# The second FFN layer of a parallel transformer block in seven block products, with its weights streamed from DRAM

## The chip, the cores and the metric

The kernel runs on one core of one Trainium2 chip. The metric is the device time of one execution in microseconds (us), lower being better; before the change it is 2092.24 us, the median of two runs (2092.05 and 2092.44). The engines named below are PE (matrix products), DVE (vector), ACT (scalar), POOL (GpSimd) and SP, which issues nearly all DMAs. Each engine works through its own list of instructions in order, and waits where an operand or a buffer is not ready.

## The reference

For 16 sequences of 512 tokens with 256 features: layer normalisation, then eight-head causal attention and a three-layer feed-forward network (FFN) side by side, both added to the input. The FFN's weights are booleans that stand for +1 and -1.

```python
def _conn_dense(kernel_bool, x):
    w = jnp.where(kernel_bool, jnp.float32(1.0), jnp.float32(-1.0))
    return x @ w
h = jnp.concatenate([x, -x], axis=-1)
h = s0 * _conn_dense(k0, h)          # 512 -> 1024
h = jax.nn.relu(h) * 2
h = s1 * _conn_dense(k1, h)          # 1024 -> 1024
h = jax.nn.relu(h) * 2
h = s2 * _conn_dense(k2, h)          # 1024 -> 256
...
xn = _layernorm(x, axis=-1)
x = x + _L0_attn_ref(xn, wq, wk, wv, wo) + _L0_ffn_ref(xn, k0, k1, k2, s0, s1, s2)
```

## The kernel before

**Batches and slots.** The 16 sequences are called batches `b`, the 8 heads `h`. One head of one batch is a slot, `g = 8b + h`, 128 slots in all. A slot scores head g row block by row block (`score_row`, L500: PE product `s`, DVE masked row minimum, ACT exponential, DVE reciprocal, POOL scaling), transposes its probabilities block by block (`turn`, L520: DVE, then a trip through DRAM, `bounce_p` out and `pT` back), projects q and k of head g+1 (`project_qk`, L457), multiplies probabilities and values of head g-1 (`attend`, L562), and adds the output projection of head g-2 to the sums `y` (`project_o`, L596). Around that, pieces of the FFN and of the next batch's layer norm are laid by hand.

**Who sets the order.** PE, SP and POOL run in the order in which the code issues (manual scheduling, L843). DVE and ACT are ordered by the framework; `behind` (L245) ties some of their instructions to a slot. An order once built is fixed.

**Rope.** `rotate` (L395) turns q and k: ACT copies with the halves swapped, DVE multiplies by the cosine, POOL by the sine (L405), POOL adds (L407). On POOL the order in a slot is: row block 0, sine of q, sum qT, row blocks 1 and 2, sine of k, row block 3, sum kT. The next slot's first score product needs that kT.

**Seven products.** q, k and v are already computed as 2x2 blocks in seven products in Strassen's manner (`seven_products`, L421), on PSUM tiles `pa` and `pb`. ACT copies intermediate states `ca`, `cb`, `cu` out before PE accumulates on, DVE adds the rest. The weights' sums (`w7_sb`, `wv7_sb`) are made once and stay in SBUF.

**FFN.** A float32 activation is split into two parts of the faster type fp32r, `h` and `l` (high and low), each multiplied by the same exact weights. Layer one, `ffn0(b, f)` (L619), makes one of eight feature blocks of 128: four products of 512 columns, then ACT makes the high part with a ReLU (L634) and DVE the low part (L635), both from PSUM. Layer two, `ffn1(b, f)` (L638), makes one output block with 16 products of 512 columns (eight chunks, two parts, L642); layer three, `ffn2` (L655), adds 8 products of 256 columns to `y` (L588). Eight blocks f of layer two lie in the eight slots, one slot late: each slot holds one block. `slot_of_head_0` (L718) holds all of layer one for its batch, `slot_of_head_1` (L774) and `slot` (L815) the rest. PSUM tiles of the products come from a pool `mm` of three.

**DMA.** SP sends, in each slot: the bounce out, four pT back, one `w1` block of 512 KB for layer two (`load_w1`, L158). The pT transfers wait for the bounce to land; everything after them on SP waits too. w1 was made from booleans in batch 0 (`make_w1`, L229) and written to `w1_dram`. All other weights stay in SBUF.

Of the kernel before, what the change touches and what calls it, by code (L numbers as in the profile page):

```python
# [22 lines left out]
def kernel(  # L23
# [92 lines left out]
    w7_sb = wpool.tile([P, 7, HD], F32, tag="w7", name="w7_sb")  # L116
# [4 lines left out]
    wv7_sb = wpool.tile([P, 7, NG, VN], F32, tag="wv7", name="wv7_sb")  # L121

    def load_w(engine, sb, w, h0, h1):
        engine.dma_start(
            sb[:, :, h0 * D : h1 * D],
            w[:, h0:h1, :].rearrange("(c p) h d -> p c (h d)", p=P),
        )

    def load_wk(engine, h0, h1):
        load_w(engine, w7_sb[:, WK0 : WK1 + 1 : WK1 - WK0], wk, h0, h1)  # L130
# [6 lines left out]
    k2_sb = hpool.tile([P, NF1, M], U8, tag="h1l", name="k2_sb")  # L137
    wo_sb = wpool.tile([P, H, M], F32, tag="wo", name="wo_sb")

    k1s, w1s = {}, {}
    w1_dram = dram.tile([NF1, P, NF0, P], F32, tag="w1", name="w1_dram", bufs=1)

    def load_k1(f):
        k1s[f] = wpool.tile([P, NF0, P], U8, tag="k1", name=f"k1_{f}", bufs=2)
        nc.sync.dma_start(k1s[f], k1.rearrange("(c p) f -> p c f", p=P)[:, :, ts(f, P)])

    def load_wv(gv):
        for c, places in enumerate(((A11, A21), (A12, A22))):  # L150
            nc.sync.dma_start(
                wv7_sb[:, places[0] : places[1] + 1 : places[1] - places[0], gv],
                wv[ts(c, P), gv * VH : (gv + 1) * VH, :].rearrange(
                    "p (i h) d -> p i (h d)", i=2
                ),
            )

    def load_w1(b, f):  # L158

        if (b, f) == (1, 0):  # L160
            nc.sync.dma_start(w1_dram[NF1 - 1], w1s[0, NF1 - 1].bitcast(F32))
        if 0 < b < B:
            w1s[b, f] = wpool.tile([P, NF0, P], F32R, tag="w1", name=f"w1_{b}_{f}", bufs=2)
            nc.sync.dma_start(w1s[b, f].bitcast(F32), w1_dram[f])
        elif b == 0:
            if f:
                nc.sync.dma_start(w1_dram[f - 1], w1s[0, f - 1].bitcast(F32))
            if f + 1 < NF1:
                load_k1(f + 1)

    load_w(nc.sync, w7_sb[:, WQ0 : WQ1 + 1], wq, 0, 2)
    load_wk(nc.scalar, 0, 2)
    nc.sync.dma_start(cos_sb, cos_t)
    nc.scalar.dma_start(sin_sb, sin_t)
    load_wv(0)
# [4 lines left out]
    for h0, h1 in ((2, 4), (4, H)):  # L180
        load_w(nc.sync, w7_sb[:, WQ0 : WQ1 + 1], wq, h0, h1)
        load_wk(nc.sync, h0, h1)
    load_k1(0)
    for gv in range(1, NG):
        load_wv(gv)
    xs[1] = load_x(1)
    nc.sync.dma_start(wo_sb, wo.rearrange("h d m -> d h m"))
    nc.sync.dma_start(k2_sb, k2.rearrange("(c p) f -> p c f", p=P))
# [14 lines left out]
    w2_sb = wpool.tile([P, NF1, M], F32R, tag="w2", name="w2_sb")  # L203
    sg_sb = cpool.tile([P, 3], F32, tag="sg", name="sg_sb")
    sg2_sb = cpool.tile([P, 3], F32, tag="sg2", name="sg2_sb")
    nsg_sb = cpool.tile([P, 3], F32, tag="nsg", name="nsg_sb")
    ab_sb = cpool.tile([P, 3], F32, tag="ab", name="ab_sb")
    c_sb = cpool.tile([P, 1], F32, tag="c", name="c_sb")

    def make_scales():  # L210
        neg = small.tile([P, 3], F32, tag="neg", name="neg", bufs=1)
        nc.vector.tensor_scalar(neg, s_sb, 0.0, None, ALU.is_lt)
        nc.vector.tensor_scalar(sg_sb, s_sb, 0.0, None, ALU.is_gt)
        nc.vector.tensor_tensor(sg_sb, sg_sb, neg, ALU.subtract)
        nc.vector.tensor_scalar(sg2_sb, sg_sb, 2.0, None, ALU.mult)
        nc.vector.tensor_scalar(nsg_sb, sg_sb, -1.0, None, ALU.mult)
        nc.vector.tensor_tensor(ab_sb, s_sb, sg_sb, ALU.mult)
        nc.vector.tensor_scalar(c_sb, ab_sb[:, 0:1], ab_sb[:, 1:2], 8.0, ALU.mult, ALU.mult)
        nc.vector.tensor_tensor(c_sb, c_sb, ab_sb[:, 2:3], ALU.mult)
# [9 lines left out]
    def make_w1(f, reduced, raised):  # L229
        t = w1s[0, f] = wpool.tile([P, NF0, P], F32R, tag="w1", name=f"w1_0_{f}", bufs=2)  # L230
        if f % 2:
            behind(nc.scalar.activation(
                t, k1s.pop(f), AF.Identity, bias=nsg_sb[:, 1:2], scale=sg2_sb[:, 1:2]
            ), raised)
        else:
            behind(nc.vector.tensor_scalar(
                t, k1s.pop(f), sg2_sb[:, 1:2], sg_sb[:, 1:2], ALU.mult, ALU.subtract
            ), reduced)

    def make_w2(reduced):  # L240
        behind(nc.vector.tensor_scalar(
            w2_sb, k2_sb, sg2_sb[:, 2:3], sg_sb[:, 2:3], ALU.mult, ALU.subtract
        ), reduced)
# [139 lines left out]
    def project_v_directly(b, gv):  # L383
        new_v(b, gv)
        for c in range(NT):
            pv = ps_mm.tile([P, T], F32, tag="mm", name=f"pv_{b}_{gv}_{c}")
            for i, places in enumerate(((A11, A12), (A21, A22))):
                for m in range(NM):
                    nc.tensor.matmul(  # L389
                        pv[:, ts(i, VN)], tokens(xnTs[b], m)[:, c], wv7_sb[:, places[m], gv],  # L390
# [18 lines left out]
    def project_qk_directly(g, engine):  # L409

        for name, places in (("q", (WQ0, WQ1)), ("k", (WK0, WK1))):
            pq = ps_mm.tile([P, T], F32, tag="mm", name=f"p{name}_{g}")
            for m in range(NM):
                nc.tensor.matmul(  # L414
                    pq, w7_sb[:, places[m], ts(g, D)], tokens(xnTs[0], m),
                    start=(m == 0), stop=(m == NM - 1),
                )
# [3 lines left out]
    def seven_products(name, b, product):  # L421
# [13 lines left out]
        t = tts[b]  # L435
        product(pa[:, :n], A11, xn_half(b, 0, 0), start=True, stop=False)
        product(pa[:, n:], A12, xn_half(b, 1, 0), start=False, stop=True)
        ca = work.tile([P, T], F32, tag="ca", name=f"ca_{name}", bufs=1)
        nc.scalar.copy(ca, pa)  # L439
        product(pb[:, n:], S1, t[:, 0], start=True, stop=False)  # L440
        product(pb[:, :n], A22, t[:, 3], start=False, stop=True)
# [3 lines left out]
        product(pa[:, :n], S2, t[:, 1], start=False, stop=False)  # L445
# [3 lines left out]
        product(pb[:, n:], S4, xn_half(b, 1, 1), start=False, stop=True)  # L449
        product(pa[:, :n], A21, t[:, 2], start=False, stop=True)  # L450
# [3 lines left out]
             cb.rearrange("p (i t) -> p i t", i=2)),  # L454
        )

    def project_qk(g):  # L457
# [5 lines left out]
        def product(out_, place, right, **marks):  # L463
            nc.tensor.matmul(  # L464
                out_, w7_sb[:, place, ts(h, D)], right, skip_group_check=True, **marks
            )

        for sums in seven_products(f"qk_{g}", b, product):
# [11 lines left out]
    def project_v(b, gv, t):  # L480
# [6 lines left out]
        def product(out_, place, right, **marks):  # L487
            nc.tensor.matmul(  # L488
                out_, right[:, t], wv7_sb[:, place, gv], skip_group_check=True, **marks
            )  # L490

        for sums in seven_products(f"v_{b}_{gv}_{t}", b, product):
# [69 lines left out]
    def attend(g):  # L562
# [7 lines left out]
        nc.vector.tensor_copy(oT, po)  # L570
# [25 lines left out]
    def project_o(g):  # L596
        b, h = divmod(g, H)
        for _ in add_y(b, oTs.pop(g), wo_sb[:, h, :]):
            pass
# [17 lines left out]
    h0s, h1s = {}, {}  # L617

    def ffn0(b, f):  # L619
        if f == 0:  # L620
            h0s[b] = [
                hpool.tile([P, NF0, T], F32R, tag=f"h0{n}", name=f"h0{n}_{b}") for n in "hl"
            ]
        ph = ps_mm.tile([P, T], F32, tag="mm", name=f"ph0_{b}_{f}")
# [8 lines left out]
        hi, lo = h0s[b][0][:, f, :], h0s[b][1][:, f, :]  # L633
        nc.scalar.activation(hi, ph, AF.Relu)  # L634
        nc.vector.scalar_tensor_tensor(lo, ph, 0.0, hi.bitcast(F32), ALU.max, ALU.subtract)  # L635
        yield

    def ffn1(b, f):  # L638
        ph = ps_mm.tile([P, T], F32, tag="mm", name=f"ph1_{b}_{f}")
        for c in range(NF0):  # L640
            for i in range(2):
                nc.tensor.matmul(  # L642
                    ph, w1s[b, f][:, c], h0s[b][i][:, c, :],
                    start=(c == 0 and i == 0), stop=(c == NF0 - 1 and i == 1),
                )
                if c < NF0 - 1 or i == 0:
                    yield
        hi = hpool.tile([P, T], F32R, tag="h1h", name=f"h1h_{b}_{f}")
        lo = hpool.tile([P, T], F32R, tag="h1l", name=f"h1l_{b}_{f}")
        nc.scalar.activation(hi, ph, AF.Relu)  # L650
        nc.vector.scalar_tensor_tensor(lo, ph, 0.0, hi.bitcast(F32), ALU.max, ALU.subtract)
        h1s[b, f] = (hi, lo)
        yield

    def ffn2(b, f):  # L655
        for r in h1s.pop((b, f)):
            yield from add_y(b, r, w2_sb[:, f, :])
# [12 lines left out]

# [3 lines left out]
    def scale_first():  # L674
        for places, scale, engine in (
            ((WQ0, WQ1), Q_SCALE, nc.gpsimd), ((WK0, WK1), K_SCALE, nc.scalar),
        ):
            for place in places:
                cols = w7_sb[:, place, : 2 * D]
                if engine is nc.scalar:  # L680
                    engine.mul(cols, cols, scale)
                else:
                    engine.tensor_scalar(cols, cols, scale, None, ALU.mult)

    def make_w7(w, scale1, scale2, reduced=None, raised=None, engine=nc.vector):

        for place, scale in ((A22, -scale2), (A21, scale2), (A11, scale1), (A12, scale1)):
            if scale != 1.0:
                behind(nc.scalar.mul(w[place], w[place], scale), raised)
        for out_, a, c in (  # L690
            (S1, A21, A22), (S2, S1, A11), (S4, A12, S2), (A21, A11, A21)
        ):
            tied = reduced if engine is nc.vector else None
# [238 lines left out]
```

## Time and profile before

| What | Value |
|---|---|
| median of two runs | 2092.24 us |
| profiled execution: its time, its span | 2091.51 us, 2089.7 us |
| granted TensorE clock | 0.999 |
| DVE, ACT, POOL busy, share of span | 67%, 52%, 49% |
| DMA: bytes of the SP queue, share of 16 engines | 281.34 MB, 45.3% |

A batch in the middle, by the starts of the first score product of each slot (the timeline of PE, us from the span's start):

| Slot (head) | start | length |
|---|---|---|
| 0 (all of layer one) | 1046.95 | 22.11 |
| 1 (half of a v projection) | 1069.06 | 15.83 |
| 2 (v) | 1084.89 | 16.72 |
| 3 (v) | 1101.61 | 16.72 |
| 4, 5, 6 | 1118.33 | 41.10 together |
| 7 (v) | 1159.43 | |

"Busy" is time in which an engine has an instruction in flight; for PE, whose products are pipelined, the distance from start to start is the cost, and mean durations overlap. An "idle before" with an arrow names what the engine waited for.

### The profile page before, as it was taken

To read this page: it belongs to the slowest core of one execution; us is meant where nothing else is said; L and a number is where in the kernel's file an instruction comes from. 1 tells how busy PE (TensorE), PEld (TensorE's weight loads), DVE (VectorE), ACT (ScalarE), POOL (GpSimd) and SP (SyncE) were. 2 spreads that over 40 slices of the span, in tenths; PEclk is the share of its full clock that TensorE was granted. 3 is DMA by queue.
4 is the path that set the end of the run, shared out by engine and by line. 5 is a ranking of instruction groups with operands and counts; after the bars stand their busy time and mean duration, and the time that the engine had idled before them with its cause. 6 is when DMAs were issued, how large, how long until landed. Compare 5 with 4: busy or idle time off the path is not lost.

```text
span 2089.7 us, 30265 instructions
## 1 busy us (share of the span) xinstructions
PE 2075.6 (99%) x9856; PEld 1730.4 (83%) x9856; DVE 1399.6 (67%) x3653; ACT 1084.7 (52%) x2418; POOL 1023.7 (49%) x1090
## 2 busy tenths in 40 slices
PE   8999999999999999999999999999999999999999
PEld 5888888888888888888888888888888888888887
DVE  7767666676666766667666676766667666676654
ACT  6555555555545555455554555555555554555543
POOL 5754445545454454444544455444554545545443
PEclk9999999999999999999999999999999999999999
DMA  6544535445444354444435444454453544534344
GB/s 181 158 141 125 159 111 155 129 126 149 124 139 139 123 142 126 149 139 122 143 114 161 127 136 130 126 159 116 137 148 113 153 116 140 158 114 139 106 139 129
DMA packets 162158, 284.33 MB, mean 136 GB/s; under 512 B 25168, under 2 KB 126544, under 8 KB 162000
## 3 DMA queue, kind: packets, MB, share of 16 engines
q1 hardware_dynamic: 160976, 281.34, 45.3%
q8 instruction: 78, 1.28, 0.3%
q10 hardware_dynamic: 1024, 1.05, 0.2%
q14 instruction: 80, 0.66, 0.1%
HBM read 178.00 MB, written 104.33 MB: 135 GB/s over the span
## 4 chain that ended last, share of the span: by engine, by line
PE 98%; DVE 1%; POOL 0%; DMA 0%; issue 0%; ACT 0%; SPq 0%; POOLq 0%; DVEq 0%; ACTq 0%
PE ph L642 22%; PE y L588 16%; PE po L543 13%; PE s L505 13%; PE pa_qk L464 10%; PE pb_qk L464 8%; PE ph L627 6%; PE pa_v L488 5%; PE pb_v L488 4%; PE pv L389 0%; DMA w_sb<-in_L_attn_wq_dram 0%; PE pq L414 0%; PE pk L414 0%; POOL w_sb L694 0%; DVE p L508 0%
## 5 line engine op out<-in xcount | busy, mean ns | idle before, releaser
L516 POOL TENSOR_SCALAR p<-p,rl 128x128 f32<-128x128 f32 (+3 forms) x512 | 296.9, 585 | 730.7 <-DVE rl L515 725.9
L642 PE MATMUL ph<-h0h,w 128*128 128x512 f32 x1024 | 519.7, 507 | 0.0
L642 PE MATMUL ph<-h0l,w 128*128 128x512 f32 x1024 | 411.3, 402 | 0.0
L505 PE MATMUL s<-kT,qT 128*128 128x128 f32 (+3 forms) x1024 | 359.3, 432 | 0.3 <-POOL kT L407 0.2
L513 ACT ACTIVATE p<-p,least 128x128 f32<-128x128 f32 (+3 forms) x512 | 286.4, 560 | 123.2 <-DVE least L508 118.1
L405 POOL TENSOR_TENSOR swq<-swq,sin_sb 128x512 f32<-128x512 f32 x127 | 197.7, 1557 | 297.3 <-ACT swq L400 295.8
L524 DVE STREAM_TRANSPOSE z<-p 128x128 f32<-128x128 f32 (+3 forms) x512 | 242.2, 493 | 93.4 <-POOL p L516 89.6
L543 PEld LDWEIGHTS po<-pT,v 128*128 128x128 f32 x1536 | 271.1, 190 | 37.6
L543 PE MATMUL po<-pT,v 128*128 128x256 f32 (+1 forms) x1536 | 298.6, 344 | 0.0
L508 DVE CUSTOM_DVE_ANT_0 p<-s,causal 128x128 f32<-128x128 f32 (+3 forms) x512 | 243.8, 484 | 14.9 <-PE s L505 14.9
L642 PEld LDWEIGHTS ph<-h0h,w 128*128 128x128 f32 x1024 | 193.1, 189 | 73.1 <-issue 26.9
L642 PEld LDWEIGHTS ph<-h0l,w 128*128 128x128 f32 x1024 | 193.3, 189 | 72.7 <-issue 26.8
L588 PE MATMUL y<-wo_sb,oT 128*128 128x256 f32 x1024 | 241.7, 379 | 0.0
L505 PEld LDWEIGHTS s<-kT,qT 128*128 128x128 f32 x1024 | 193.4, 189 | 33.7 <-POOL kT L407 0.6
L588 PEld LDWEIGHTS y<-wo_sb,oT 128*128 128x128 f32 x1024 | 193.9, 189 | 28.7
L439 ACT COPY ca_qk<-pa_qk 128x512 f32<-128x512 f32 x126 | 73.7, 585 | 274.4 <-PE pa_qk L464 274.4
L650 ACT ACTIVATE h1h<-ph 128x512 fp32r<-128x512 f32 x128 | 76.5, 597 | 253.0 <-PE ph L642 245.6
L515 DVE RECIPROCAL rl<-l 128x1 f32<-128x1 f32 x512 | 78.8, 154 | 142.3 <-ACT p L513 139.8
L407 POOL TENSOR_TENSOR kT<-kT,swk 128x512 f32<-128x512 f32 x127 | 169.4, 1334 | 0.1
L407 POOL TENSOR_TENSOR qT<-qT,swq 128x512 f32<-128x512 f32 x127 | 163.8, 1290 | 10.0
L405 POOL TENSOR_TENSOR swk<-swk,sin_sb 128x512 f32<-128x512 f32 x127 | 166.4, 1310 | 0.0
L399 ACT COPY swq<-q 64x512 f32<-64x512 f32 x126 | 77.9, 618 | 169.9 <-DVE q L474 169.9
(113 smaller groups left out, 3571.5 us busy)
## 6 DMA issues: line engine op xcount, KB each, us to landing
bounce_p<-z SPq DMA_DIRECT2D x128, 640.0 KB, 2.9
pT<-bounce_p SPq DMA_DIRECT2D x512, 160.0 KB, 3.3
w<-w_dram SPq DMA_DIRECT2D x120, 512.0 KB, 5.0
x_sum<-in_L_attn_x_dram SPq DMA_DIRECT2D x16, 512.0 KB, 6.1
x<-in_L_attn_x_dram SPq DMA_DIRECT2D x60, 128.0 KB, 6.2
bounce_x<-zx SPq DMA_DIRECT2D x15, 512.0 KB, 6.5
xnT<-bounce_x SPq DMA_DIRECT2D x60, 128.0 KB, 5.8
out_dram<-x_sum SPq DMA_DIRECT2D x15, 512.0 KB, 4.4
```

The lines of the kernel that those rows point to most:

```text
L405: engine.tensor_tensor(sw, sw, sin_sb, ALU.mult)
L407: engine.tensor_tensor(rt, rt, sw, ALU.add)
L464: nc.tensor.matmul(out_, w7_sb[:, place, ts(h, D)], right, skip_group_check=True, **marks)
L488: nc.tensor.matmul(out_, right[:, t], wv7_sb[:, place, gv], skip_group_check=True, **marks)
L505: nc.tensor.matmul(ps[:, :n], qT[:, ts(ic, P)], kT[:, :n], start=True, stop=True)
L508: reduced = nc.vector.tensor_tensor_reduce(out=p, in0=ps[:, :n], in1=causal[:, T - n :], scale=1.0, scalar=3e38, op0=ALU.add, op1=ALU.min, ...
L513: raised = nc.scalar.activation(p, p, AF.Exp, bias=least, scale=-1.0, accum_out=l)
L516: nc.gpsimd.tensor_scalar(p, p, rl, 1.0, ALU.mult, ALU.mult)
L524: behind(nc.vector.transpose(zs[:, :, block(ic, 0) : block(ic + 1, 0), :].rearrange("p j c a -> p c j a"), p.rearrange("p (c j a) -> p c j ...
L543: nc.tensor.matmul(po[:, (ics[0] - first) * P : (ics[-1] + 1 - first) * P], v[:, jc], pT[:, :, at[0] : at[-1] + 1 : max(at[-1] - at[0], 1) ...
L588: nc.tensor.matmul(ys[b][c // 2][:, c % 2, :], lhsT[:, ts(c, P)], rhs, start=(y_done[b][c] == 0 and c % 2 == 0), stop=(y_done[b][c] == N_Y ...
L642: nc.tensor.matmul(ph, w1s[b, f][:, c], h0s[b][i][:, c, :], start=(c == 0 and i == 0), stop=(c == NF0 - 1 and i == 1),)
```

## The change

1. **Layer two in pairs.** `ffn1(b, i)` makes blocks i and i+4 together in seven block products. Each is 4 chunks x 2 parts of 256 columns: 56 products of 256 columns for two blocks, where 32 of 512 columns stood. The four pairs lie in slots 2, 4, 5 and 7 (`PAIR_SLOTS`); slots 0, 1, 3 and 6 hold none. ffn2 of a pair (16 products) is in the slot after it.
2. **Sums of the activations.** `ffn0` keeps only the ReLU on ACT, into a float32 tile `h0r` of eight 256-column places. New `split_h0(b, c)`, four times in slot 0, makes four differences on POOL, then for the three plain and the four difference places the high part on ACT and the low part on DVE. `h0r` shares its buffers (one for even, one for odd chunks) with the layer-two weights.
3. **Sums of the weights.** In batch 0 each pair's seven weight blocks are made (ACT, DVE, POOL) and written to DRAM in two parts: A11, A12, S1, A22 (1 MB) and S2, S4, A21 (768 KB). Later batches load both parts of a pair. The first part is loaded in the slot before the pair, placed on SP ahead of that slot's bounce; the second at the beginning of the pair's own slot (pair 0), or of the slot after the previous pair's.
4. **Other weights streamed.** q and k weights with their sums: 448 KB for each slot; v weights: 896 KB, two for each batch; `wo`: 128 KB for each slot; `w2`: 256 KB for each pair. None stays in SBUF.
5. **Smaller.** The copy of the attention output (`oT` in `attend`) goes from DVE to ACT. Loads of x and the statistics for a batch are made earlier by several slots. All sums of weights are on POOL.

```diff
-    def ffn1(b, f):
-        ph = ps_mm.tile([P, T], F32, tag="mm", name=f"ph1_{b}_{f}")
-        for c in range(NF0):
-            for i in range(2):
-                nc.tensor.matmul(
-                    ph, w1s[b, f][:, c], h0s[b][i][:, c, :],
-                    start=(c == 0 and i == 0), stop=(c == NF0 - 1 and i == 1),
-                )
...
+    def split_h0(b, c):
+        hi, lo = (t[:, c] for t in h0s[b])
+        r = h0rs.pop(c)
+        for out_, p, q in ((T1, X12, X11), (T2, X22, T1), (T3, X22, X12), (T4, T2, X21)):
+            nc.gpsimd.tensor_tensor(r[:, out_], r[:, p], r[:, q], ALU.subtract)
+        for part in (slice(X11, T1), slice(T1, X12)):
+            nc.scalar.copy(hi[:, part], r[:, part])
+            nc.vector.tensor_tensor(
+                lo[:, part], r[:, part], hi.bitcast(F32)[:, part], ALU.subtract
+            )
+
+    def ffn1(b, i):
+        hi, lo = h0s[b]
+        def product(out_, place, x, start, stop):
+            for c in range(NC):
+                for n, t in enumerate((hi, lo)):
+                    nc.tensor.matmul(
+                        out_, w1s[b, i, place][:, c], t[:, c, x], start=start and not c + n,
+                        stop=stop and c == NC - 1 and n == 1, skip_group_check=True,
+                    )
+        for sums in seven_products(f"h_{b}_{i}", product):
+            if sums is None:
+                yield
...
+        nc.vector.tensor_tensor(first, *sums[0], ALU.add)
+        nc.vector.tensor_tensor(second, *sums[1], ALU.add)
+        nc.vector.tensor_tensor(both, *sums[2], ALU.add)
+        for t, r in enumerate(copies):
+            nc.scalar.activation(h1h[:, t], r, AF.Relu)
+            nc.vector.scalar_tensor_tensor(
+                h1l[:, t], r, 0.0, h1h[:, t].bitcast(F32), ALU.max, ALU.subtract
+            )
...
+    PAIR_SLOTS = (2, 4, 5, 7)
+    def begin(g):
...
+            load_w7(g + 2)
+        if g <= N_SLOTS:
+            load_wo(g - 1)
...
+            else:
+                load_w1(b, behind_pair + 1, 1)
...
+        if i is not None:
+            load_w2(b, i)
+        if h == 2:
+            if b:
+                load_w1(b, 0, 1)
+                load_wv7(b, 1)
...
     def slot_of_head_0(g):
...
                 some(qk, 1)
-                rest(l0[ic - 2])
+                rest(l0[(ic - 2) * NC])
         rest(qk)
         turn(g, reduced)
+        split_h0(b, 0)
         project_o(g - 2)
-        rest(l0[2], l0[3])
+        rest(l0[1], l0[NC + 1])
+        split_h0(b, 1)
         attend(g - 1)
...
+        rest(l0[2], l0[NC + 2])
+        split_h0(b, 2)
+        rest(l0[3], l0[NC + 3])
+        split_h0(b, 3)
```

## The prediction

> **What bounds the kernel now.** I read in this order: the page's busy shares, its chain of waits, PE's waits, then PE and POOL slot by slot in the timeline, and last the DMA by microsecond.
>
> ```profile
> span 2089.7 us, 30265 instructions
> ...
> PE 2075.6 (99%) x9856; PEld 1730.4 (83%) x9856; DVE 1399.6 (67%) x3653; ACT 1084.7 (52%) x2418; POOL 1023.7 (49%) x1090
> ...
> PE 98%; DVE 1%; POOL 0%; DMA 0%; issue 0%; ACT 0%; SPq 0%; POOLq 0%; DVEq 0%; ACTq 0%
> ```
>
> PE bounds everything; in steady state it never waits. Two prices come from the chain around 1000 us (start, length, what):
>
> ```profile
> 1003.65 0.93 PE y L588 x8
> 1005.88 0.92 PE ph L642 x4
> ```
>
> A 512-column fp32r product costs 0.230 us, a 256-column one 0.93/8 = 0.117: half the width is half the price, though each loads other weights. One 256-column float32 product (two records) costs 0.43, a slot's four scores 0.22, 0.43, 0.65, 0.86.
>
> But POOL is nearly as tight within a slot. The slot of head 6 starts at 1016.53 (its first score):
>
> ```profile
> 1020.66 1.57 POOL L405 TENSOR_TENSOR swq<-swq,sin_sb 128x512 f32<-128x512 f32 x1 [2.15 <-ACT swq L400]
> ...
> 1027.47 1.26 POOL L407 TENSOR_TENSOR kT<-kT,swk 128x512 f32<-128x512 f32 x1
> ...
> 1030.23 0.38 PE L505 MATMUL s<-kT,qT 128*128 128x128 f32 x2
> ```
>
> kT is ready 12.2 us after the slot's start; the slot lasts 13.7. The one short slot of the startup shows the limit, 12.1 us after the previous first score (37.64):
>
> ```profile
> 49.77 0.49 PE L505 MATMUL s<-kT,qT 128*128 128x128 f32 x2 [0.20 <-POOL kT L407]
> ```
>
> **The change part by part.**
>
> *PE.* Layer two: 2048 x 0.230 = 471 us goes, 3584 x 0.117 = 419 comes: 52 us gained, all on the bounding engine; nothing else of PE changes. PE alone would need per slot, adding instructions by these prices: slot 0 18.4, slot 1 12.1, 2 15.6, 3 17.0, 4 15.6, 5 17.5, 6 11.0, 7 18.6: 125.8 us for a batch, before 129.2. I now ask of each slot what else must fit.
>
> *Slot 6.* PE needs 11.0, POOL's chain 12.2 to 12.6 (the third score stays, the fourth comes 0.8 later behind the output projection). It takes 12.4: 1.4 lost.
>
> *Slots 0 and 1.* `split_h0` issues 16 POOL differences of 128x256. The nearest row, the weight sums of batch 0, gives four in 3.2 us (POOL, L694, 3.04 to 3.38). So 12.8 us of POOL follow kT in slot 0. High parts: eight ACT copies of 768 and 1024 columns; nearest rows: 1134 ns for 1024 (L224), 0.71 for 512 from SBUF (L352); so 0.86 and 1.13. Low parts: DVE 256 and 512 columns take 0.42 and 0.69, so 0.96 and 1.23. ReLU 0.60 as now.
>
> The instruction order of the changed program decides. ACT reads: ReLU of block 1; high differences of chunk 0; ReLU 5; both high copies of chunk 1; oT; ReLU 2; ReLU 6; plain copy of chunk 2; ReLU 3; high differences of chunk 2; ReLU 7; ca of the next q/k; both high copies of chunk 3; only then cb of the next q/k and the exponential. So ReLUs that POOL needs stand behind copies that need POOL, and PE's three PSUM tiles are emptied by those ReLUs. With the slot's first score at 0: kT at 11.8, as now; split 0 ends 15.0, its copy 16.2, ReLU 5 16.85; split 1 (16.9 on) 19.3, copy 20.5, oT 21.1, ReLU 2 21.7, ReLU 6 22.3; split 2 24.9, copy 26.1, ReLU 7 26.7; ca 27.3, split 3 29.1, copy 30.3, cb 30.9. PE: block 3 waits for ReLU 5, block 7 for ReLU 2, the next pb for ReLU 3 (23.8), so slot 1 starts at 24.7, not 18.4; its first q/k accumulation waits for ca, S4 for cb, and q/k end at 31.8, where PE alone would be at 21.6. From there sine of q starts 1.7 later (as in the fence) and kT follows 8 later: slot 2 starts at 41.6, PE alone 30.5.
>
> DVE's low parts read two SBUF operands beside POOL's differences. The row:
>
> ```profile
> L372 DVE TENSOR_TENSOR tt<-xnT 128x256 f32<-128x256 f32 x32 | 32.9, 1031 | 0.0
> ...
> L372 DVE TENSOR_TENSOR tt<-xnT,tt 128x256 f32<-128x256 f32 x16 | 6.4, 399 | 0.0
> ```
>
> The same work takes 1031 ns where POOL is busy and 399 where not. [...] Slots 0 and 1 take 43 us (bounds 38 and 48); now they take 37.9. DVE's and ACT's load alone (28 and 30 of 30.5 us) would nearly fill PE's time too.
>
> *Slot 2, DMA.* The second weight part of pair 0 can be loaded only here, its buffer having held h0r. On SP stand before it: pT of slot 1, which waits for that slot's bounce, then the output, w7, wo, w2. In slot 1 the last transpose comes 0.7 after row block 3, kT 1.3 after it, so the bounce leaves 0.5 us before slot 2 starts, not 3.6 as now (1081.25 against 1084.89). The bounce takes 2.9; at +2.4 pT begins; 0.66+0.52+0.46+0.13+0.26+0.79 = 2.8 MB must move. What such a burst moves:
>
> ```profile
> 1085.00:1086.00 1.00, 1.00 (x9) 0.95 (x8) 0.94 (x4) 0.86 (x2) 0.00 (x0) 1.00 0.72 189
> 1086.00:1087.00 1.00, 1.00 (x9) 0.95 (x8) 0.16 (x1) 0.47 (x3) 0.38 (x1) 1.00 1.05 260
> 1087.00:1088.00 1.00, 1.00 (x6) 0.87 (x5) 0.81 (x2) 0.30 (x1) 0.00 (x0) 1.00 1.01 215
> 1088.00:1089.00 1.00, 1.00 (x5) 0.75 (x4) 1.00 (x3) 0.96 (x3) 0.00 (x0) 1.00 1.07 316
> 1089.00:1090.00 1.00, 1.00 (x5) 0.75 (x4) 1.00 (x4) 0.99 (x2) 0.97 (x1) 1.00 1.13 424
> 1090.00:1091.00 1.00, 1.00 (x6) 0.84 (x6) 1.00 (x2) 0.82 (x3) 0.92 (x2) 1.00 0.84 324
> ```
>
> The last column is GB/s: mean 288 over 6 us with all engines busy. So 9.7 us plus about 1 to start and finish: +13. PE needs S2 at +7.2: 6 us lost. [...] I take the trace, 6 (bounds 2 and 8). Over a batch the loads are no bound: 14.9 MB of weights instead of 4.2 make some 450 MB, at 281.34 MB in 45.3% about 73% of the engines' time.
>
> *Pair slots 4, 5, 7 and slot 3.* ACT gains ca, cb, cu (1.5 us) per pair, DVE three adds and two low parts of 0.69 to 0.86 (3 us) where two low parts stood; 9 us lie between the last score and the first y product that needs them: nothing lost. Second parts of later pairs are sent a slot ahead or, in slot 5, some 2 us early by the same rate: nothing; if slower, 1 us each. The oT copy (0.69 on DVE, 0.6 on ACT) is covered by the slot until its y product; in slot 0 it is counted above. w7, wo and w2 come a slot ahead and are hidden; uncovered, each costs 2 to 5 us.
>
> *Sum of a batch.* 43 + 21.6 + 17.0 + 15.6 + 17.5 + 12.4 + 18.6 = 145.7, before 129.2: 16.5 longer, 15 times: 247 us.
>
> *Batch 0.* POOL additionally makes w7 (4 sums of 128 columns, about 1.8 us each head), v sums 3.2 twice, w1 sums 4 x 1.3 for each pair. In slots 0 and 1: 1.8 x 2 and 3.2 more among the splits, then 10 behind kT that hold up sine of q in slot 2; slot 6 starts behind 7. By the same reckoning slot 2 starts near 71 us instead of 49.77, slot 8 about 30 later than now, less what its own pairs save. I take 28 (bounds 12 and 40). The tail saves 2.
>
> Total: 2089.7 + 247 + 28 - 2 = 2363 as span; the run's own time is 1.8 above its span, the median 0.7 above that. Of two estimated stalls I have more room to err downwards; I put 2355.
>
> **The rivals.** *All is hidden (faster).* If the low-priority work found gaps as it does now (PE waits 9 us in the whole run), only PE counts: 2092 - 52 = 2040. For it: DVE reached 12.1 busy of 13.7 us in slot 6 without a stall. Against: ACT's fixed order. It decides where the four splits, from kT to cb, take under about 8 us; I count 19. Chance 8%.
>
> *The gain is spent (within 2%).* Slots 0 and 1 lose 3, slot 6 1, slot 2 nothing, batch 0 10: about 2060 to 2110. Chance 6%.
>
> *One of two.* Only the POOL and ACT chain (slot 2 in time: 15 x 6 less, 2265) or only the weights (15 x 12 less, 2175). Between 2134 and 2265; 19%.
>
> *Both, as forecast.* 2265 to 2450: 67%. A half-width product that costs more than half, so that the change gives no PE time, is spoken against by the y row; it would add 52.
>
> **How the numbers follow.** 2% is about what a measurement of this kernel tells from no change: below 2050 faster, above 2134 slower. Faster 0.08, same 0.06, slower 0.86. The range from 2190 to 2430 leaves out the first two cases and the low end of the third, and a few in a hundred above.
>
> **What would show it.** In the profile after: PE busy share clearly below 99%; PE waiting for ACT at layer one (ReLU) and at q/k S4 in slots 0 and 1, about 10 us a batch; the L706 groups on POOL at 0.75 to 1.0 us each; PE waiting for the DMA of the second weight part in slot 2; slot 6 waiting for kT; slot 2 beginning 41 to 45 us after slot 0. I am wrong if slots 0 and 1 take under 34, or if no product waits for a weight transfer.

## The result and the profile after

The changed kernel takes 2497.19 us (median of 2 runs, 2496.5 to 2497.89), 1.1935 times the time before (95% interval 1.1884 to 1.1987): 405 us more, where the forecast was 263 more. The sign and the two stalls that the forecast named were right; the size was not, and two further losses were not in it.

The page of the changed kernel: span, busy shares, the granted clock in 40 slices, the chain by engine.

```profile
span 2496.1 us, 35132 instructions
...
PE 2191.5 (88%) x11392; PEld 1822.4 (73%) x11392; DVE 1595.6 (64%) x3726; ACT 1368.0 (55%) x2884; POOL 1294.4 (52%) x1380
...
PEclk8998999999999899998999989999998999989999
...
PE 46%; POOL 17%; ACT 11%; DVE 10%; DMA 8%; issue 6%; SPq 1%; ACTq 0%; POOLq 0%; DVEq 0%
```

PE, 98% of the chain before, is 46% of it now; POOL, ACT, DVE and DMA are links of the chain. The clock row has 8s, where a granted clock of 1.0 would show 9s. What PE waits for (total us, times, longest):

```profile
PE ph L689 <- ACT h0r L696: 100.2, 31, 12.5
PE pa_h L720 <- DMA w<-w_dram: 87.8, 20, 6.5
PE pb_qk L517 <- ACT cb_qk L487: 37.1, 18, 2.6
PE s L558 <- POOL kT L442: 21.8, 16, 1.8
PE pa_h L720 <- ACT cu_h L491: 12.9, 16, 3.4
```

The first and third are slots 0 and 1 (layer one's ReLUs, the copies of q/k), the second is slot 2 (the late weight), the fourth slot 6. The fifth, the copy `cu_h`, is in slot 7; I had not counted it at all.

Slot lengths, from first score to first score on PE, mean of batches 1 to 15:

| slot | before | forecast | after | after less forecast |
|---|---|---|---|---|
| 0 and 1 | 37.9 | 43.0 | 43.6 | +0.6 |
| 2 | 16.7 | 21.6 | 24.3 | +2.7 |
| 3 | 16.7 | 17.0 | 17.75 | +0.75 |
| 4 | 13.7 | 15.6 | 16.4 | +0.8 |
| 5 | 13.7 | 17.5 | 18.2 | +0.7 |
| 6 | 13.6 | 12.4 | 12.4 | 0 |
| 7 | 16.7 | 18.6 | 21.1 | +2.5 |

That is 8.1 us a batch more than forecast, some 121 us in 15 batches. Batch 0 (start of slot 0 to start of slot 8) grew from 118.3 to 160.2 us, by 42 instead of 28. Together 135 us: the whole miss in the span (2496.1 against 2363, or 133).

How slots 0 and 1 look on POOL in batch 8 (start, length, what, idle before and its releaser). The slot starts at 1263.27:

```profile
1273.25 1.29 POOL L442 TENSOR_TENSOR kT<-kT,swk 128x512 f32<-128x512 f32 x1
1274.49 4.34 POOL L706 TENSOR_TENSOR h0r<-h0r 128x256 f32<-128x256 f32 x5
1279.87 3.29 POOL L706 TENSOR_TENSOR h0r<-h0r 128x256 f32<-128x256 f32 x3 [1.03 <-ACT h0r L696]
1285.30 4.36 POOL L706 TENSOR_TENSOR h0r<-h0r 128x256 f32<-128x256 f32 x5 [2.14 <-ACT h0r L696]
1290.69 3.48 POOL L706 TENSOR_TENSOR h0r<-h0r 128x256 f32<-128x256 f32 x3 [1.04 <-ACT h0r L696]
```

Sixteen differences in four pieces; before three of them POOL waits for a ReLU, 4.2 us in all. kT is ready 11.3 us after the slot's start (11.8 assumed). This is the ring of the forecast.

PE in the same slot showed what I had not thought of:

```profile
1285.28 0.79 PE L689 MATMUL ph<-xh,w_sb 128*128 128x512 f32 x1 [4.28 <-ACT h0r L696]
1285.87 0.63 PE L689 MATMUL ph<-xl,w_sb 128*128 128x512 f32 x1
1286.29 0.63 PE L689 MATMUL ph<-xh,w_sb 128*128 128x512 f32 x1
```

Behind the wait of 4.28 us the products follow each other at 0.42 us instead of 0.23. The granted clock changes only at multiples of 3.41 us in this trace, so the stretches below are laid on that grid; the first five lie around that wait, the last three in slot 2 of the same batch, which starts at 1306.50 (length, busy of PE with count, then granted clock, DMA share, GB/s):

```profile
1277.80:1281.21 3.41, 1.63 (x6) 1.00 0.94 220
1281.21:1284.62 3.41, 0.00 (x0) 0.50 0.41 145
1284.62:1288.03 3.41, 2.75 (x7) 0.50 0.00 0
1288.03:1291.45 3.42, 3.42 (x10) 0.50 0.00 0
1291.45:1294.86 3.41, 2.22 (x10) 1.00 0.73 250
...
1315.34:1318.75 3.41, 0.00 (x0) 1.00 1.05 409
1318.75:1322.17 3.42, 2.90 (x11) 0.50 1.08 380
1322.17:1325.58 3.41, 3.41 (x24) 1.00 0.81 324
```

The granted clock falls to 0.50 in slot 0 and in slot 2 (in stretches of 4 us of slot 2 it shows as a mean of 0.84 and 0.73), and PE is busy in part of that time: a wait seemed to be followed by a second loss.

### The profile page after: what moved, and what is told of

Its sections match the earlier page's. It is cut to its first block, busy times and chain, and to the rows that moved or that the text cites. A ratio compares the mean times of both kernels' runs of the same rounds, so it can differ in the third digit from the quotient of the medians.

```text
span 2496.1 us, 35132 instructions
## 1 busy us (share of the span) xinstructions
PE 2191.5 (88%) x11392; PEld 1822.4 (73%) x11392; DVE 1595.6 (64%) x3726; ACT 1368.0 (55%) x2884; POOL 1294.4 (52%) x1380
## 3 DMA queue, kind: packets, MB, share of 16 engines
q1 hardware_dynamic: 213392, 452.42, 56.1%
## 4 chain that ended last, share of the span: by engine, by line
PE 46%; POOL 17%; ACT 11%; DVE 10%; DMA 8%; issue 6%; SPq 1%; ACTq 0%; POOLq 0%; DVEq 0%
POOL h0r L706 9%; PE pa_h L720 8%; PE y L641 8%; PE po L596 7%; PE pa_qk L517 5%; DMA w<-w_dram 4%; PE s L558 4%; PE pb_qk L517 4%; PE pb_h L720 4%; PE pa_v L541 3%; PE pb_v L541 2%; DVE tt L407 2%; ACT h0h L708 2%; POOL p L569 2%; DVE p L561 2%
## 5 line engine op out<-in xcount | busy, mean ns | idle before, releaser
L720 PE MATMUL pa_h<-h0h,w 128*128 128x256 f32 x1024 | 295.8, 321 | 100.7 <-DMA w<-w_dram 87.8
L720 PEld LDWEIGHTS pa_h<-h0h,w 128*128 128x128 f32 x1024 | 204.8, 200 | 133.4 <-issue 100.1
L709 DVE TENSOR_TENSOR h0l<-h0r,h0h 128x768 fp32r<-128x768 f32 (+1 forms) x128 | 162.3, 1268 | 181.1 <-ACT h0h L708 178.9
L706 POOL TENSOR_TENSOR h0r<-h0r 128x256 f32<-128x256 f32 x256 | 243.1, 975 | 66.7 <-ACT h0r L696 64.1
L720 PE MATMUL pa_h<-h0l,w 128*128 128x256 f32 x1024 | 265.2, 292 | 0.0
L641 PE MATMUL y<-wo,oT 128*128 128x256 f32 x1024 | 261.1, 401 | 0.7 <-ACT oT L623 0.7
L641 PEld LDWEIGHTS y<-wo,oT 128*128 128x128 f32 x1024 | 204.2, 204 | 33.6 <-ACT oT L623 1.1
L720 PE MATMUL pb_h<-h0h,w 128*128 128x256 f32 x768 | 218.7, 321 | 0.0
L720 PEld LDWEIGHTS pa_h<-h0l,w 128*128 128x128 f32 x1024 | 205.7, 201 | 11.3 <-issue 9.8
L720 PE MATMUL pb_h<-h0l,w 128*128 128x256 f32 x768 | 189.2, 283 | 0.0
L442 POOL TENSOR_TENSOR qT<-qT,swq 128x512 f32<-128x512 f32 x127 | 180.0, 1417 | 9.9
```

The lines of the kernel that those rows point to most:

```text
L442: engine.tensor_tensor(rt, rt, sw, ALU.add)
L641: nc.tensor.matmul(ys[b][c // 2][:, c % 2, :], lhsT[:, ts(c, P)], rhs, start=(y_done[b][c] == 0 and c % 2 == 0), stop=(y_done[b][c] == N_Y ...
L706: nc.gpsimd.tensor_tensor(r[:, out_], r[:, p], r[:, q], ALU.subtract)
L720: nc.tensor.matmul(out_, w1s[b, i, place][:, c], t[:, c, x], start=start and not c + n, stop=stop and c == NC - 1 and n == 1, skip_group_c ...
```

## The experiments

Two stalls were to be told apart first, the ring in slots 0 and 1 and the late weight in slot 2; then what each consists of; then the losses in slots 3 to 7. All times are medians in us; the kernel before took 2091.4 to 2092.5 beside these runs. `filler`, `cover` and `best` were run four times, with 5.7, 18.4 and 5.2 us between lowest and highest; the others once, so that a difference of some 20 us in the time alone says little, and the slot lengths of the traces stand beside it.

### The late weight alone: early

```diff
-            h0rs[chunk] = wpool.tile(
-                [P, 8, half_tokens], F32, tag=f"w1{chunk % 2}", name=f"h0r_{b}_{chunk}"
+            h0rs[chunk] = (hpool if chunk % 2 else wpool).tile(
+                [P, 8, half_tokens], F32, tag=("w10", "h1")[chunk % 2], name=f"h0r_{b}_{chunk}"
             )
...
+        h1 = hpool.tile([P, 2, 2, T], F32R, tag="h1", name=f"h1_{b}_{i}")
+        h1h, h1l = h1[:, 0], h1[:, 1]
...
+        if h == 1:
+            load_w1(b, 0, 1)
...
         if h == 2:
             if b:
-                load_w1(b, 0, 1)
                 load_wv7(b, 1)
```

> Edit: the raw layer-one tiles of chunks 1 and 3 lie where h1 lies (free at that time), so that the buffer of the second weight part of a pair is free from slot 7 on, and pair 0's part is sent at the start of slot 1 instead of slot 2. Nothing else moves. If the late weight is a matter of the buffer and of the place in the queue: no product in slot 2 waits for a weight transfer, the slot goes from 24.3 us to 16 to 17 (PE alone 15.6), 15 times 7.5 us or some 112 us less: about 2385. If the streamed weights are simply too many bytes, the lateness moves to another slot or stays: over 2450. If the lowered clock seen after the wait is caused by the wait, slot 2's products also go back to the full clock; if not, they stay slow and the slot does not get below 18.

It took 2398.45: 99 us less. Slot 2 fell from 24.3 to 16.4 us, and no product in it waits for a weight. Slots 0 and 1 stayed (43.9). The same bytes are streamed, so it was the place of the transfer, not the amount. Slot 5 rose from 18.2 to 19.0 us, where the second part of another pair comes late (PE waits for it nine times, 13.4 us in the run): about as much as is missing from the expected 112 us.

### The ring's parts: nodiff and order

```diff
-        for out_, p, q in ((T1, X12, X11), (T2, X22, T1), (T3, X22, X12), (T4, T2, X21)):
-            nc.gpsimd.tensor_tensor(r[:, out_], r[:, p], r[:, q], ALU.subtract)
-        for part in (slice(X11, T1), slice(T1, X12)):
-            nc.scalar.copy(hi[:, part], r[:, part])
+        for part, src in ((slice(X11, T1), r[:, X11:T1]), (slice(T1, X12), r[:, X11 : T1 + 1])):
+            nc.scalar.copy(hi[:, part], src)
```

> Edit: POOL's 16 differences of the layer-one output per batch are left out (the high and low parts of the four difference blocks are taken from other blocks of the same tile, so ACT and DVE copy as much as before). The differences are the part left out. If POOL's work in the ring is the cost: no ReLU stands behind a copy that waits for POOL, slots 0 and 1 together go from 43.6 us to 31 to 34 (PE alone 30.5), 15 times 11 and some 12 in batch 0: about 2320. If ACT's and DVE's copying alone is too much (28 and 30 us of work in 30.5), slots 0 and 1 stay above 38 and the time above 2410. Slot 2 stays near 24, since its weight comes as late as before or its lateness grows by nothing.

It took 2308.54: slots 0 and 1 fell to 32.4 us (PE alone 30.5), slot 2 stayed at 24.3. The kernel leaves out the differences. ACT's and DVE's copies by themselves cost 1.9 us a batch at most; POOL's differences, and what stands behind them, cost 11.2 us a batch and 15.7 in slots 0 and 1 of batch 0.

With the differences kept and only ACT's order changed (`differences` and `copies` are the two halves of `split_h0`; the third argument puts the copy of the difference blocks behind that instruction; the last lines stand in slot 1, behind its first exponential):

```diff
-        split_h0(b, 0)
+        differences(b, 0)
         project_o(g - 2)
         rest(l0[1], l0[NC + 1])
-        split_h0(b, 1)
+        copies(b, 0, relus[NC + 1])
+        differences(b, 1)
...
+                if b:
+                    copies(b, 3, raised)
```

> Edit: only ACT's order. The copy of a chunk's difference blocks is put behind the ReLUs of the next chunk, and that of the last chunk behind the first exponential of slot 1; POOL has the same 16 differences, no buffer is added. If it is ACT's order that makes POOL and ACT wait for each other in turn: POOL runs its 16 differences nearly without a break, 15.6 us from kT at 11.8 to about 27.4, the next kT follows at about 32.5 to 34, slots 0 and 1 take 34 to 37 us instead of 43.6, and the time is 2370 to 2400. If POOL's throughput alone sets it, or the exclusion of DVE and POOL, slots 0 and 1 stay above 41 and the time above 2455.

It took 2421.24: 76 us less, slots 0 and 1 39.3 us. The ring is gone (the next kernel's profile, which has the same order, shows the sixteen differences in one run), but the gain is smaller than expected. Why is in that profile too.

### Both: both

The two edits together.

> Edit: the early weight and ACT's order together. If the two stalls are independent: their gains add, some 112 and 110 to 128 us: 2255 to 2280, and the mean granted clock rises from 0.949 to above 0.97. If slot 2's lateness only followed from slots 0 and 1 being long (or the other way round), the sum is less: above 2330.

It took 2314.78: 182 us less than the changed kernel; the two alone gave 99 and 76. The stalls are independent, as far as single runs tell (175 against 182). The granted clock's mean rose from 0.949 to 0.98. My number was lower by 35 to 60 us, for the reason that POOL's timeline shows (slot start 1179.95), then the groups (count, busy, mean ns, idle before):

```profile
1191.17 16.83 POOL L708 TENSOR_TENSOR h0r<-h0r 128x256 f32<-128x256 f32 x16
```

```profile
L708 POOL TENSOR_TENSOR h0r<-h0r 128x256 f32<-128x256 f32 x256 | 261.0, 1046 | 6.0 <-ACT h0r L696 1.0
...
L717 DVE TENSOR_TENSOR h0l<-h0r,h0h 128x1024 fp32r<-128x1024 f32 x64 | 91.5, 1429 | 104.8 <-ACT h0h L714 104.7
...
L717 DVE TENSOR_TENSOR h0l<-h0r,h0h 128x768 fp32r<-128x768 f32 x64 | 90.7, 1417 | 1.2 <-ACT h0h L714 1.0
```

POOL does its sixteen differences in one piece now, nearly without a gap. Each got longer instead: 1046 ns a difference (975 in the changed kernel), and DVE's low parts of 768 columns take as long as those of 1024. Either that is what the work takes, or the two engines hold each other up.

### DVE and POOL beside each other: nolow, dvediff, alldve

```diff
-            nc.vector.tensor_tensor(lo[:, part], r[:, part], hi.bitcast(F32)[:, part], ALU.subtract)
...
-                for n, t in enumerate((hi, lo)):
+                for n, t in enumerate((hi, hi)):
```

> Edit on the kernel with the early weight and ACT's order (2314.8 us): DVE's eight low parts of layer one's output per batch are left out and the high parts are multiplied in their place, so PE has as many products. If DVE's instructions with two SBUF inputs and POOL's differences exclude each other: POOL's differences fall from 1046 ns to 0.75 to 0.85 us, the unbroken run of 16 from 16.8 to 12 to 13.6, slots 0 and 1 from 39.3 to 35.5 to 36.5, the time by some 45 to 60 us to 2255 to 2270. If a POOL difference simply takes 1.05 us: slots 0 and 1 stay above 38.5 and the time above 2300.

It took 2241.87: 73 us less than with the low parts, more than expected; this kernel leaves the low parts out. The group of POOL's differences in it:

```profile
L708 POOL TENSOR_TENSOR h0r<-h0r 128x256 f32<-128x256 f32 x256 | 182.5, 739 | 6.0 <-ACT h0r L696 1.0
```

739 instead of 1046 ns, 4.9 us a batch; slots 0 and 1 fell by 4.8 us to 34.5. The trace of the kernel with the low parts says the same from within: of its 256 differences the 102 with no low part beside them take 737 ns (median), the 154 with one beside them 1437. So DVE's low parts slow POOL's differences, and on the path in full. Whether the two exclude each other, as the expectation supposes, or only slow each other, these runs do not separate.

```diff
-        for out_, p, q in ((T1, X12, X11), (T2, X22, T1), (T3, X22, X12), (T4, T2, X21)):
-            nc.gpsimd.tensor_tensor(r[:, out_], r[:, p], r[:, q], ALU.subtract)
+        for out_, p, q in ((T3, X22, X12), (T1, X12, X11), (T2, X22, T1), (T4, T2, X21)):
+            engine = nc.vector if out_ == T3 else nc.gpsimd
+            engine.tensor_tensor(r[:, out_], r[:, p], r[:, q], ALU.subtract)
```

> Edit on the same kernel (2314.8 us): one of the four differences of each chunk is taken from POOL and given to DVE, same result. If POOL's run of 16 differences is what sets slots 0 and 1 now: it shrinks to 12, some 12 to 13 us, slots 0 and 1 go from 39.3 to 35 to 37, the time to 2255 to 2285. If the exclusion between DVE and POOL eats it, or DVE's fixed order makes POOL wait: the mean of POOL's differences rises above 1.15 us or gaps appear, slots 0 and 1 stay above 38, the time above 2298.

It took 2290.97, between the two expectations: 24 us less, slots 0 and 1 37.9. A quarter of the differences gone from POOL did not give a quarter of its time: the rest still take 1036 ns, POOL now waits 20.0 us in the run before them (6.0 without the edit), and DVE needs 918 ns for its one. Sharing the work between the two engines gained little here.

With all sixteen on DVE (`nc.vector` in that line):

> Edit on the kernel with the early weight and ACT's order (2314.8 us): all sixteen differences of a batch are taken from POOL and given to DVE, same result. If the exclusion of DVE and POOL is a large part of slots 0 and 1 (a difference measured 1046 ns on POOL beside DVE's low parts, 739 without them; a low part 1.42 us): DVE does a difference in 0.4 to 0.6 us with POOL quiet, a low part falls below 1.2 us, slots 0 and 1 go from 39.3 to 33.5 to 36, the time to 2225 to 2265. If DVE has no room (it is busy 27.6 of 39.3 us there now): slots 0 and 1 stay above 37.5, the time above 2290.

It took 2254.68: 60 us less, with nothing left out of the computation. Slots 0 and 1: 35.4 us. Its groups on DVE:

```profile
L708 DVE TENSOR_TENSOR h0r<-h0r 128x256 f32<-128x256 f32 x256 | 115.0, 489 | 3.7 <-DVE h0r L708 0.5
...
L717 DVE TENSOR_TENSOR h0l<-h0r,h0h 128x1024 fp32r<-128x1024 f32 x64 | 78.4, 1224 | 0.0
...
L717 DVE TENSOR_TENSOR h0l<-h0r,h0h 128x768 fp32r<-128x768 f32 x64 | 61.2, 956 | 0.0
```

DVE does differences and low parts in 254.6 us, where it took 182.2 for the low parts alone beside POOL's 261.0. The engine with more to do is the better place here, for two reasons that this run does not separate: no difference on POOL runs beside it any more (a low part of 768 columns takes 956 ns instead of 1417), and it needs 489 ns for a difference where POOL needs 739 even with the low parts gone.

### The clock: filler

On the changed kernel itself, `fill` issues 16 products of pair 0's A11 weights with the high parts, into the attention's PSUM tile, ahead of those that wait for the late weight:

```diff
+            if h == 2 and b and ic == NT - 1:
+                fill(b, 16)
             some(tile, 1)
```

> Edit on the changed kernel as it is: in slot 2 of every batch but the first, 16 full-width products on data that is ready (into the PSUM tile of the attention, which nobody reads) stand before the S2 products that wait for the late weight: about 3.7 us of work inside a wait of 4 to 6.5 us, nothing else. Their results are not used. If the wait itself lowers the TensorE clock (granted 0.73 to 0.84 behind it in slot 2): the rest of the wait is under 3 us, the clock stays near 1, and slot 2 goes from 24.3 us to 22.3 to 23, the time falls by 20 to 30 us to 2467 to 2477, although work was added. If the clock falls for another reason, or the products behind the wait are slow only because the transfer is still running: slot 2 stays at 24.3 or grows, the time is 2495 to 2510.

It took 2466.09 (4 runs; ratio to the kernel before 1.1779, interval 1.1759 to 1.1799, against 1.1884 to 1.1987 of the changed kernel). With work added, the time fell by 31 us, slot 2 from 24.3 to 22.4. PE in slot 2 of batch 8, which starts at 1293.88, and its stretches on the grid of the clock:

```profile
1301.47 4.22 PE L753 MATMUL pf<-h0h,w 128*128 128x512 f32 x16
1307.51 0.36 PE L720 MATMUL pa_h<-h0h,w 128*128 128x256 f32 x1 [1.82 <-DMA w<-w_dram]
1307.70 0.28 PE L720 MATMUL pa_h<-h0l,w 128*128 128x256 f32 x1
1307.82 0.28 PE L720 MATMUL pa_h<-h0h,w 128*128 128x256 f32 x1
```

```profile
1302.75:1306.17 3.42, 2.94 (x13) 1.00 1.00 398
1306.17:1309.58 3.41, 2.07 (x13) 1.00 1.02 380
1309.58:1312.99 3.41, 3.41 (x24) 1.00 0.92 366
```

The weight lands 13.6 us after the slot's start, in the mean of 15 batches no earlier than without the filler (13.6 in both); what changed is that PE waited 1.8 us instead of 4.6 (means 1.8 and 5.4) and the clock stayed at 1.00, although the DMA engines were still busy (shares 1.02 and 0.92). The products follow each other at 0.12 us; in the changed kernel, behind the wait, at 0.21:

```profile
1319.27 0.55 PE L720 MATMUL pa_h<-h0h,w 128*128 128x256 f32 x1 [4.61 <-DMA w<-w_dram]
1319.62 0.41 PE L720 MATMUL pa_h<-h0l,w 128*128 128x256 f32 x1
1319.83 0.41 PE L720 MATMUL pa_h<-h0h,w 128*128 128x256 f32 x1
```

So the slow clock is a consequence of PE's idleness, and its going saves 1.9 us of slot 2. In two of the 15 batches it fell in this run too; there the rest of the slot behind the weight's landing takes 10.0 and 10.2 us, in the first batch without a fall 8.6.

### The copy cu: cover, wfirst

In the seven-product form S2 goes into one half of a PSUM tile, ACT copies it (`cu`), and A21 is added into the same half. Where only S4 stands between, PE waits. The copy `cb` stands in the same way before S4 in q and k. Slot 7 of the kernel of both edits, then slot 4 of the changed kernel:

```profile
1309.74 0.28 PE L728 MATMUL pb_h<-h0l,w 128*128 128x256 f32 x1
1310.63 0.39 PE L728 MATMUL pa_h<-h0h,w 128*128 128x256 f32 x1 [0.61 <-ACT cu_h L491]
```

```profile
1347.19 0.60 PE L517 MATMUL pa_qk<-tt,w 128*128 128x256 f32 x2
1347.85 0.70 PE L517 MATMUL pb_qk<-xnT,w 128*128 128x256 f32 x2
1348.59 0.70 PE L517 MATMUL pa_qk<-tt,w 128*128 128x256 f32 x2
```

In slot 4 no wait is printed, but two products that cost 0.43 us lie 0.66 and 0.74 us apart: `cb_qk` and then `cu_qk` release the next ones.

Put other products between:

```diff
                 some(l2, 2 * NT)
+                if h in (2, 4):
+                    project_o(g - 2)
                 some(qk, 1)
...
         elif h == H - 1:
+            project_o(g - 2)
             rest(tile)
             attend(g - 1)
             for v in vs:
                 some(v, 1)
-            project_o(g - 2)
...
+        elif h in (2, 4):
+            attend(g - 1)
+            rest(tile)
```

> Edit on the same kernel (2314.8 us): only PE's order in slots 2, 4 and 7. The output projection is put between the S2 and the S4 products of q/k in slots 2 and 4, the attention of the head before between S2 and S4 of the pair there, and in slot 7 the output projection between S2 and S4 of the pair. If it is the copy cu on ACT that PE waits for when no other work stands behind S2: slots 2 and 4 go from 16.4 to 15.7 to 16.0, slot 7 from 20.9 to 19.8 to 20.3, together 1.5 to 2.3 us a batch, 2280 to 2292. If the half-width products themselves are slower than half, or the wait only moves to the next PSUM tile: less than 0.5 us a batch, above 2307.

The slots did as the first theory says: 2 and 4 fell from 16.4 to 15.8, 7 from 20.9 to 20.0. The time did not: 2317.07 (4 runs, 2306.64 to 2325.06; the slots are those of the fastest) beside 2314.78 (one run). Slot 5 had grown from 18.1 to 19.6, and PE's wait for weight transfers from 5.2 to 17.0 us in the run. A slot that is shorter leaves the next weight less time. Slot 3 had grown from 17.75 to 18.1: by the starts of its products PE waits 0.37 us more for `ca_qk` at its beginning, and the same 0.37 in slot 5; both stay in the next two kernels, and no run took them away. In the next kernel the late weight goes first:

```diff
         else:
+            if b < B and h - 1 in PAIR_SLOTS:
+                load_w1(b, PAIR_SLOTS.index(h - 1) + 1, 1)
             load_w7(g + 2)
...
-            else:
-                load_w1(b, behind_pair + 1, 1)
```

> Edit on the kernel with PE's order changed in slots 2, 4 and 7 (2317.1 us median, slot 5 19.6 and slot 3 18.1 us): the second weight part of a pair is sent ahead of the next head's w7 and of wo at a slot's start; nothing else moves. If that kernel's 2.1 us a batch were lost again in slot 5 to that part coming late: slot 5 goes from 19.6 to 17.7 to 18.3, the wait of PE for a weight transfer falls from 17 to under 6 us, the time to 2285 to 2300. If slot 5 is long for another reason (a PSUM tile, a copy): it stays above 19 and the time above 2308.

It took 2288.24 (one run), slot 5 18.15: as expected for the late transfer, for which PE now waits 0.7 us in the run. That slot 5 is no shorter than in the changed kernel is the 0.37 us for `ca_qk`. Some of the wait went to w7 instead (PE waits for it ten times in the run, 10.0 us in all).

### All together: best

> All together: early weight, ACT's order (in the first slot of the run too), PE's order in slots 2, 4 and 7, second weight parts first, and all differences on DVE. If the causes are separate: the sum of a batch is 34.5 + 15.8 + 18.0 + 15.8 + 18.1 + 12.4 + 20.0 = 134.6 us, against 129.2 before and 153.9 in the changed kernel, batch 0 some 8 us shorter: about 2200, range 2175 to 2235, still slower than before by 4 to 7%. If it is below 2134, slots 0 and 1 have fallen under 30.5, which PE alone needs, and my count of PE is wrong.

It took 2222.86 (4 runs, 2219.96 to 2225.11; 1.0624 times the time before, interval 1.0606 to 1.0642). A batch takes 135.9 us (134.6 expected), batch 0 153.7 instead of 160.2 (8 us less expected, 6.5 found; ACT's order in the first slot of the run was tried in no run by itself). What PE waits for in it:

```profile
PE pb_qk L517 <- ACT h0r L696: 21.3, 15, 1.4
PE s L558 <- POOL kT L442: 17.5, 14, 2.9
PE ph L689 <- ACT h0r L696: 12.6, 16, 1.6
PE pa_v L541 <- ACT cu_v L491: 9.8, 15, 0.7
```

Of the 405 us that the change cost, 274 come back by order, places of buffers and choice of engine. It is still slower than before: slots 0 and 1 stand at 35.4 where PE alone needs 30.5, slot 6 at 12.5 where it needs 11.0, slots 3 and 7 at 1.1 and 1.6 above theirs. The waits that are left come to 10 us a batch; two thirds of them would have to go before the change gains anything.

## Why the prediction fell short

Of the 142 us between 2355 and 2497, slots 3, 4, 5 and 7 are 71, slot 2 is 40, slots 0 and 1 are 9, batch 0 is 14, and 8 are what I took off 2363 because two stalls seemed more likely too long than too short.

*PE's gain: the price is nearly confirmed, the gain is not realised.* A 256-column product follows the next at 0.120 us (0.117 taken), a full-width one at 0.232. PE's own need fell by some 45 us instead of 52 at these prices, and no slot is bound by it alone except nearly 2 and 4 of the last kernel.

*Slots 0 and 1, 43 forecast, 43.6 measured: right in sum, and in mechanism; its parts were mis-sized.* ReLUs behind copies that wait for POOL: 4.3 us (order). DVE's low parts beside POOL's differences: the 2 us that the 43 holds for them on top of 41.6 are an estimate of mine that no run shows. What the runs showed: in the changed kernel a difference took 975 ns, without the low parts 739 (nolow), 3.8 us over sixteen; with the ring taken away it is 4.8 on the path. Against these 1.8 us too few stand 1.0 us too many for the differences themselves (0.8 us each, not 0.739) and 0.5 for kT (11.8, not 11.3). That the sum is right to 0.6 us is luck. My row for the two engines did not show what I said: the 399 ns were no case of an idle POOL, which was busy scaling for 228 of them; what ran beside the slow ones (1175 and 955 ns near 1021 us) was POOL's sine and sum. The lowered clock (granted 0.50 from 1281.21 to 1291.45 us in batch 8) is a third part that I did not have; how much of these slots it costs beside the ring was not measured by itself.

*Slot 2, 21.6 forecast, 24.3 measured: the stall was right, its consequence missing.* The weight landed at +12.8 us in batch 8, +13.6 in the mean (+13 forecast). The burst before it moved a mean of 348 GB/s from 1310 to 1319 us, not my 288, whose first microsecond had the engines busy for 0.72 of it; it landed no earlier because some 3.1 MB moved by then, not 2.8, and SP issued it only 7.0 us into the slot (1313.48). PE comes to S2 0.8 us later than I had, for the small waits for `cb` and `cu` ahead of it. The step that failed is "6 us lost", which priced a wait at its length: the clock behind it adds 1.9 us (filler), and the whole excess over what the slot takes with the weight in time is 7.9 (early).

*Slots 3, 4, 5 and 7, "nothing lost": this is the step of the sum that failed most, 4.75 us a batch, 71 us in the run.* I asked whether ACT's and DVE's additional work fits into the slot, and it does; I did not ask which product is next behind each copy. With other products put between, slots 2, 4 and 7 each became 0.6 to 0.8 us shorter (cover), in slots 2 and 4 about half of it a wait for `cb` and half for `cu`. The rest I read from the starts of PE's products in the changed kernel's trace: what lies between two starts beyond the price of the product is put down to what released the next one. Of the 4.75 us, slot 3 has 0.7, behind the copies and the addition of v (`cu_v`, DVE's L549); slot 4 0.6, behind `cb_qk` and `cu_qk`; slot 7 1.9, behind `cu_h` (0.9), `cu_qk` (0.65) and `cu_v` (0.35), and 0.4 more because the clock fell 1.8 us into the slot in three of 14 batches (22.3 us instead of 20.7). Slot 5 has 0.5 behind the second weight part, which PE waits for in five of 15 batches (eight take 17.67 us); it was foreseen as "if slower, 1 us each". The last 0.6 are PE's own need at 0.120 us a product. What remains in slots 3 and 7 behind the copies of v, q and k was taken away by no run.

*Slot 6: 12.4, as forecast, waiting 1.3 us for kT.*

*Batch 0: slot 2 begins at 71.33 us, forecast 71; the lengthening was 42, not 28.* Slots 0 and 1 of it were right to half a us. Behind them, slots 2 to 7 took 113.1 us (92.8 before), 20 more, where I had left 7, counting on what batch 0's own pairs save; they saved nothing, since these slots take together what they take in every batch (110.1) and 3 us more; slots 3 and 6 (19.0 and 16.8 us) are 1.3 and 4.4 us longer, beside the weight sums on POOL, slot 2 2.2 shorter. Whether POOL's sums are the cause was not tested: only slots 0 and 1 of batch 0 were taken apart by runs (nodiff).

*DMA as a whole: 452.42 MB as forecast (450), at 56.1% of the engines' time, not 73.* No bound over a batch, as said.

## What to carry to other kernels

A wait on PE is not priced by its length alone: the products behind it can run at half the clock, in the changed kernel, after its first 100 us, behind all 32 stretches of 3.41 us at full clock in which PE was busy for less than 42%, and behind 7 of 19 with 42 to 52%. Filling such a wait with products whose result nobody reads can be worth more than it costs (filler: 31 us less). When halving the width of products, go through every read of a PSUM tile that the next product adds into, and ask what stands between them on PE; "it fits into the slot" answers another question. Two engines side by side can do less than two engines' work (both: a difference on POOL took 1437 ns beside a low part on DVE, 737 without): try the work on one of them (alldve: 60 us less) before dividing it (dvediff: 24).

## What the hardware showed that was not expected

In these traces the granted TensorE clock is 1.00 or 0.50, nothing else, and changes on a grid of 3.41 us. It follows how busy PE was in the stretch before, busy as the profile reckons it. In the changed kernel behind its first 100 us, PE was busy for less than 42% of a stretch at full clock 32 times, and the clock was halved behind each; for more than 52% 583 times, and behind none; in between 19 times, and behind 7. It came back behind stretches with over 83%, 39 times, and with under 81% it stayed low, 27 times. In `filler` the clock fell behind 19 of 19 stretches under 42%, 5 of 13 between and none of 617 over 52%.

So it is not the length of one wait. In slot 0 the clock fell at 1281.21, 0.2 us after the wait of 4.28 us began: the wait of 1.57 us before it had already left PE busy for 1.63 of 3.41 us. PE was back at 1.00 some 6 us after it had resumed, in slot 2 after about 3 us. In `filler` a wait of 2.23 us (batch 10) was followed by the fall and one of 3.32 us (batch 4) was not, as they lay on the grid.

In the changed kernel the clock fell in slots 0 and 2 of each of batches 1 to 15 (slot 2's mean granted clock 0.80 to 0.93). Slot 2 is the one place where the cost was measured: 31 us of 2497, 1.2% (filler).

DVE and POOL are slower beside each other on both sides: POOL's 128x256 difference took 739 ns without and 1046 beside DVE's low parts; DVE's low part of 768 columns 956 ns with POOL free of the differences and 1417 beside them.
